# A gated delta rule on one NeuronCore: how the other stages' matmul columns are dealt out between the steps of its recurrence

## The chip, the core and the metric

One core of a Trainium2 chip runs the whole program; nothing else runs beside it. The metric is the device time of one execution in microseconds (us), and lower is better. The kernel before takes 4035.74 us, the median of three runs (4035.33 to 4039.92).

The core has five engines, each with a queue of its own that is worked off in order: TensorE (PE) for matmuls and transposes, with its weight loads as a row of their own (PEld); VectorE (DVE); ScalarE (ACT); GpSimd (POOL); and SyncE (SP), whose queue only issues DMAs.

## What is computed

Three layers follow each other on x of 4 x 512 tokens with 512 channels, all in float32. The change lies in the first one, a gated delta rule with 16 heads of 128 x 128 state:

```
q, k, v = silu(conv4(x @ W.T))              # causal convolution over 4 tokens, per channel
g, beta = exp(-exp(A_log) * softplus(a + dt_bias)), sigmoid(b)
q, k    = l2norm(q), l2norm(k)              # per head
for t in range(512):                        # per sequence and head, state S is 128 x 128
    error = v[t] - g[t] * (S.T @ k[t])
    S     = g[t] * S + outer(k[t], beta[t] * error)
    o[t]  = S.T @ q[t]
o = rmsnorm(o) * norm_w * silu(x @ Wg.T)    # rmsnorm over all heads
x = x + o @ Wo.T
```

Cross attention with fake quantisation follows, then causal attention and a mixture of 8 experts. They stay as they are, apart from what is said of counts below.

## The kernel before

**Pairs.** The recurrence is computed in chunks of 128 tokens, four to a sequence (`TB`), for two heads at a time (`HG`). Sequence and two heads make a *pair* `m`; there are 32 (`NP`). A pair passes through these generators, each of which yields between pieces of work:

- `stage1(m)` (L508) projects k and q, runs the convolution (`conv`, L483: four matmuls of 512 columns at L489, ScalarE at L497, three VectorE instructions at L500, silu on ScalarE at L503), transposes k (L532), takes its norms (squares at L537; on GpSimd a power at L544 and the products L545 to L548), scales the decay matrix `em` with them on ScalarE (`scale`, L383), multiplies k by k (L562) and writes the matrix `at` (L565) to DRAM (L566), multiplies q by k (L585), and sums q's squares (L594). The inverse of q's norm is formed on GpSimd (L608, L609).
- `stage2_inverse(m)` (L622) inverts the 32 x 32 diagonal blocks in 31 steps of two instructions (L630, L631), on VectorE for even `m` and on GpSimd for odd `m`, and stores and reloads them as `T` and `X`.
- `stage2_values(m)` (L646) projects v and the gate `gs` (silu at L493), and stores q's inverse norms (L651).
- `stage3(m)` (L676) is the recurrence itself. It first joins the blocks of the inverse to 128 x 128 in four small rounds of matmuls (L690/L691, L700/L702, L713, L722), with copies out of PSUM between them: of the copies after the first two rounds, L693, L704 and L706 are on VectorE, L694 and L705 on ScalarE, two instructions each to a pair. Then it loads q's inverse norms, broadcast to all partitions (`rrow`, L728), and multiplies the two gates by them on GpSimd (L731). Then come the four chunks `c`, each a chain from PE to another engine and back: state times k (L744), `r` on VectorE (L746), the inverse times `r` (L753), `u` copied by ScalarE (L755), the state's increment (L763), the new state (L766 on ScalarE for `c` = 0, else L768 on VectorE), and the output (L771, L773). At the end VectorE multiplies the output by norm weight and gate (`og`, L782, the reader of `gs`) and by q's inverse norms (L786), ScalarE squares it (L790) and GpSimd adds it up (L791).
- `output(m)` (L796) multiplies `og` by Wo (L811) and adds on VectorE (L816). After a sequence's last pair it also ends the sequence. `prologue(b)` (L387) prepares a sequence.

**Order.** While `stage3(m)` runs, the loop at L906 hands out the work of other pairs: `output(m - 1)`, `stage1(m + 2)`, `stage2_values(m + 1)`, `stage2_inverse(m + 1)`, and in one pair of eight `prologue`. `turns` (L170) gives each of them one or two steps (the number beside it) for every one of the 15 yields of `stage3(m)`, without regard to how much TensorE work a step holds:

```
rest = turns(*rest)
for _ in stage3(m):
    next(rest, None)
run(rest)
```

This sets the order in which instructions are traced. The framework then schedules: an instruction that it takes to be ready earlier may go ahead of another on its engine, so the order of the built program is near to this one and not the same. In the built program every engine's queue is fixed and runs in order. PSUM tiles of the projections and joins come from a pool of four (`p_b`), those of the recurrence from a pool of two (`p_s`).

**The rest.** The first pair's stages run before the loop. After the loop, cross attention and causal attention are interleaved tile by tile by `weave` (L145), which uses counts of steps from the table `steps` (L142); the experts follow. `cross(0)` alone runs in the loop, beside the last pair.

Of the kernel before, what the change touches and what calls it, by code (L numbers as in the profile page):

```python
# [33 lines left out]
ALU = mybir.AluOpType  # L34
# [64 lines left out]
def decoder(ctx: ExitStack, tc: tile.TileContext, a: dict, out: bass.AP):  # L99
# [42 lines left out]
    steps = {"first": 15, "cross": 30, "qkv": 15, "rest_of": 3, "route": 8}  # L142
    steps.update((f"attention{c}", n) for c, n in enumerate((28, 32, 44, 48)))

    def weave(*gs):  # L145
# [4 lines left out]
        while todo:  # L150
            t = min(todo)
            try:
                next(t[3])
                t[5] += 1
                t[0] += t[1]
            except StopIteration:
                steps[t[4]] = max(t[5], 1)
                todo.remove(t)
            yield

# [27 lines left out]
    def transposed(src, pool, name, bufs=2):  # L188

        tp = p_b.tile([P, KD, P], F32, name="pb")  # L190
        for kd in range(KD):
            nc.tensor.transpose(tp[:, kd, :], src[:, kd * P : (kd + 1) * P], ident)
# [26 lines left out]
    def cross(i):  # L219
# [11 lines left out]
        for kd in range(KD):  # L231
            nc.tensor.matmul(pq, xT[:, kd, :], wq[:, kd, :], start=kd == 0, stop=kd == KD - 1)
# [11 lines left out]
        def scores(g0, r0, out):  # L244
# [3 lines left out]
            for g in range(2):  # L248
                for r in range(2):
                    rs = slice((r0 + r) * HD2, (r0 + r + 1) * HD2)  # L250
                    nc.tensor.matmul(ps[r][:, g, :], qT[rs, g0 + g, :], x_kT[rs, g0 + g, :], start=True, stop=True)
# [18 lines left out]
        def turned(e, out):  # L270

            for r in range(2):
                tp = p_b.tile([P, 2, 2, P], F32, name="pb")
                for g in range(2):
                    for kt in range(2):
                        nc.tensor.transpose(tp[:, g, kt, :], e[:, 2 * r + g, kt * P : (kt + 1) * P], ident)
# [5 lines left out]
        def weighted(g0, eTs):  # L282

            pa = p_b.tile([P, 2, P], F32, name="pb")
            for g in range(2):
                for kt in range(2):
                    for r in range(4):
                        h = 4 * (g0 + g) + r
                        nc.tensor.matmul(pa[r * HD2 : (r + 1) * HD2, g, :], x_val[:, kt, h * HD2 : (h + 1) * HD2], eTs[r][:, g, kt, :], start=kt == 0, stop=kt == 1)
# [13 lines left out]
        for kd in range(KD):  # L303
            nc.tensor.matmul(pw, aT[:, kd, :], wpj[:, kd, :], start=kd == 0, stop=kd == KD - 1)
# [7 lines left out]
    with ExitStack() as st:  # L312
# [74 lines left out]
        def prologue(b):  # L387
# [8 lines left out]
            for c, t in enumerate(x):  # L396
# [5 lines left out]
                for kd in range(KD):  # L402
                    nc.tensor.transpose(tp[:, kd, :], t[:, kd * P : (kd + 1) * P], ident)
# [3 lines left out]
            for c in range(TB):  # L407
                for kd in range(KD):
                    nc.tensor.matmul(pab[:, c, :], xnT[:, kd, c * P : (c + 1) * P], wab[:, kd, :], start=kd == 0, stop=kd == KD - 1)
# [28 lines left out]
            for n, m in enumerate((C_UP, C_LO, C_ONE)):  # L438
                nc.tensor.matmul(pg[:, n, :], tab_a[:, m, :], lgf, start=True, stop=True)
# [21 lines left out]
            nc.tensor.transpose(tp[:, 0, :], w.rearrange("p h i -> p (h i)"), ident)  # L461
            nc.tensor.transpose(tp[:, 1, :], gam.rearrange("p h i -> p (h i)"), ident)
# [20 lines left out]
        def conv(b, hg, p, m, wt, dst):  # L483
# [4 lines left out]
            for kd in range(KD):  # L488
                nc.tensor.matmul(pj, wt[:, kd, p * P : (p + 1) * P], xnT[:, kd, :], start=kd == 0, stop=kd == KD - 1)  # L489
# [18 lines left out]
        def stage1(m):  # L508
# [20 lines left out]
            for p in range(HG):  # L529
                tp = p_b.tile([P, TB, P], F32, name="pb")  # L530
                for c in range(TB):
                    nc.tensor.transpose(tp[:, c, :], kT[p][:, c * P : (c + 1) * P], ident)  # L532
# [24 lines left out]
            for p in range(HG):  # L557
                scale(em[p], em[p], ee, p)
                pk = p_b.tile([P, TB, P], F32, name="pb")
                for c in range(TB):  # L560
                    k_ = kT[p][:, c * P : (c + 1) * P]
                    nc.tensor.matmul(pk[:, c, :], k_, k_, start=True, stop=True)  # L562
# [9 lines left out]
            for p in range(HG):  # L572
# [10 lines left out]
                for c in range(TB):  # L583
                    cs = slice(c * P, (c + 1) * P)
                    nc.tensor.matmul(pq[:, c, :], kT[p][:, cs], q[:, cs], start=True, stop=True)  # L585
# [7 lines left out]
            for p in range(HG):  # L593
                nc.tensor.matmul(pss[p * 32 : (p + 1) * 32, :], tab_a[:, C_ONE, 0:32], sq[p], start=True, stop=True)  # L594
# [51 lines left out]
        def stage2_values(m):  # L646
# [6 lines left out]
            for p in range(HG):  # L653
# [3 lines left out]
                for c in range(TB):  # L657
                    nc.tensor.transpose(tp[:, c, :], t[:, c * P : (c + 1) * P], ident)
# [17 lines left out]
        def stage3(m):  # L676
# [11 lines left out]
            for c in range(TB):  # L688
                for p in range(HG):
                    nc.tensor.matmul(py[lo[p], c, :], ats[p][:, c, 32:64], Ts[p][:, c, 0:32], start=True, stop=True)  # L690
                    nc.tensor.matmul(py[hi[p], c, :], ats[p][:, c, 96:128], Ts[p][:, c, 64:96], start=True, stop=True)  # L691
            for p in range(HG):
                nc.vector.tensor_copy(Yd[p][32:64, :, 0:32], py[lo[p]])  # L693
# [3 lines left out]
            for c in range(TB):  # L697
                for p in range(HG):

                    nc.tensor.matmul(px[half[p], c, 64:96], Xs[p][:, c, 32:96], Yd[p][:, c, 0:32], start=True, stop=True)  # L700
                for p in range(HG):
                    nc.tensor.matmul(px[half[p], c, 0:64], Yd[p][:, c, :], odd(Xs[p][:, c, :]), start=True, stop=True)  # L702
# [747 lines left out]
```

## Time and profile before

| what | value |
| --- | --- |
| median of three runs | 4035.74 us |
| the profiled execution's own time | 4042.91 us |
| span of its first to its last instruction | 4041.2 us |
| first join matmul (L690) of the first and of the last pair | 150.5 us and 2114.3 us |
| PE, DVE, ACT, POOL busy over the span | 88%, 55%, 38%, 34% |
| granted TensorE clock over the span | 0.930 of full |

How to read the profile: times are us from the span's start, unless marked ns. A group of instructions is named by its line, engine, operation and tile, as out<-in; the arrow in `<-DVE r L746` names what ended a wait. A float32 matmul appears as two instructions and a transpose as one. "Half clock" below is a stretch in which the granted TensorE clock is 0.50.

### The profile page before, as it was taken

To read this page: it belongs to the slowest core of one execution; us is meant where nothing else is said; L and a number is where in the kernel's file an instruction comes from. 1 tells how busy PE (TensorE), PEld (TensorE's weight loads), DVE (VectorE), ACT (ScalarE), POOL (GpSimd) and SP (SyncE) were. 2 spreads that over 40 slices of the span, in tenths; PEclk is the share of its full clock that TensorE was granted. 3 is DMA by queue.
4 is the path that set the end of the run, shared out by engine and by line. 5 is a ranking of instruction groups with operands and counts; after the bars stand their busy time and mean duration, and the time that the engine had idled before them with its cause. 6 is when DMAs were issued, how large, how long until landed. Compare 5 with 4: busy or idle time off the path is not lost. (4 is left out here: it accounts for less than half of the span.)

```text
span 4041.2 us, 50395 instructions
## 1 busy us (share of the span) xinstructions
PE 3555.1 (88%) x17170; PEld 2069.9 (51%) x17170; DVE 2220.7 (55%) x5115; ACT 1523.5 (38%) x4190; POOL 1370.0 (34%) x1941
## 2 busy tenths in 40 slices
PE   5898888988998898988898899979998998898797
PEld 3455555555555555555555455545554555455343
DVE  5566656766567755767555555445544554444211
ACT  2433434344433343343433344434443444343121
POOL 1453455434453354434552211121112111211342
PEclk7899899999999999999998899989998999899898
DMA  5334333343334333243334433443334443446344
GB/s 158 104 85 114 97 100 110 102 120 95 105 86 129 107 104 104 74 141 94 102 111 138 142 123 123 123 123 123 123 123 123 129 127 112 125 156 204 76 83 91
DMA packets 391888, 465.66 MB, mean 115 GB/s; under 512 B 128451, under 2 KB 242115, under 8 KB 391440
## 3 DMA queue, kind: packets, MB, share of 16 engines
q1 hardware_dynamic: 380080, 438.03, 36.4%
q0 software_dynamic: 10112, 21.58, 2.9%
q8 instruction: 137, 2.24, 0.2%
q10 hardware_dynamic: 1440, 2.84, 0.2%
q14 instruction: 119, 0.97, 0.1%
HBM read 401.76 MB, written 64.81 MB: 115 GB/s over the span
## 5 line engine op out<-in xcount | busy, mean ns | idle before, releaser
L489 PE MATMUL pb<-xnT,w 128*128 128x512 f32 x2048 | 955.8, 606 | 0.0
L489 PEld LDWEIGHTS pb<-xnT,w 128*128 128x128 f32 x2048 | 382.4, 196 | 424.9 <-issue 420.8
L500 DVE SCALAR_TENSOR_TENSOR cv<-pb,pp,cv 128x511 f32<-128x511 f32 (+2 forms) x576 | 427.6, 742 | 156.6 <-ACT cv L497 144.3
L1049 PE MATMUL pb<-c_q,hT 128*128 128x512 f32 x768 | 370.9, 625 | 0.2 <-ACT hT L194 0.2
L630 POOL TENSOR_TENSOR iW<-iA,iT 32x31 f32<-32x31 f32 (+15 forms) x496 | 249.7, 504 | 211.2 <-DMA iA<-at_d 141.2
L811 PE MATMUL pb<-wot,og 128*128 128x512 f32 x512 | 267.1, 647 | 31.8 <-DVE og L782 26.5
L631 POOL TENSOR_TENSOR iT<-iT,iW 32x31 f32<-32x31 f32 (+15 forms) x496 | 275.1, 555 | 38.9
L1113 PE MATMUL ps<-kT,qT 128*128 128x128 f32 x1280 | 205.2, 310 | 72.4 <-ACT e L1119 72.1
L1153 PE MATMUL po<-c_o,oT 128*128 128x512 f32 x512 | 247.0, 617 | 21.2 <-DVE oT L1137 11.2
L497 ACT ACTIVATE cv<-pb,pp 128x512 f32<-128x512 f32 x192 | 148.1, 771 | 264.4 <-PE pb L489 263.9
L1113 PEld LDWEIGHTS ps<-kT,qT 128*128 128x128 f32 x1280 | 183.8, 217 | 113.0 <-ACT e L1119 92.6
L1049 PEld LDWEIGHTS pb<-c_q,hT 128*128 128x128 f32 x768 | 147.0, 201 | 163.4 <-issue 160.3
L1119 ACT ACTIVATE e<-ps,nm,rq 128x128 f32<-128x128 f32 (+3 forms) x256 | 157.5, 621 | 181.8 <-DVE nm L1117 136.8
L630 DVE TENSOR_TENSOR iW<-iA,iT 32x31 f32<-32x31 f32 (+15 forms) x496 | 177.1, 357 | 14.0 <-DMA iA<-at_d 2.4
L631 DVE TENSOR_TENSOR iT<-iT,iW 32x31 f32<-32x31 f32 (+15 forms) x496 | 178.0, 359 | 11.9
L1136 PE MATMUL po<-eT,val 128*128 128x512 f32 x320 | 168.3, 620 | 15.2 <-ACT eT L1134 11.3
L258 ACT ACTIVATE x_e<-pb,nm 128x256 f32<-128x256 f32 x256 | 118.2, 474 | 149.1 <-DVE nm L255 145.6
L544 POOL TENSOR_TENSOR rk<-ss,mhalf 128x8 f32<-128x8 f32 x32 | 53.0, 1658 | 322.8 <-DVE ss L543 322.8
L263 POOL TENSOR_SCALAR x_e<-x_e 128x1024 f32<-128x1024 f32 x64 | 68.0, 1063 | 259.0 <-ACT x_e L258 141.0
L565 DVE SCALAR_TENSOR_TENSOR at<-pb,em 128x512 f32<-128x512 f32 x64 | 44.3, 692 | 200.9 <-ACT em L383 200.5
L1153 PEld LDWEIGHTS po<-c_o,oT 128*128 128x128 f32 x512 | 92.6, 196 | 118.7 <-issue 80.9
L982 POOL TENSOR_TENSOR rope_s<-q,tab 128x128 f32<-128x128 f32 x64 | 35.3, 552 | 332.1 <-DVE q L1079 246.7
(323 smaller groups left out, 6708.5 us busy)
## 6 DMA issues: line engine op xcount, KB each, us to landing
c_o<-in_c_wo_dram SPq DMA_DIRECT2D x128, 512.0 KB, 4.3
c_q<-in_c_wq_dram SPq DMA_DIRECT2D x128, 512.0 KB, 4.7
w<-in_a_w_dram SPq DMA_DIRECT2D x124, 512.0 KB, 3.9
row<-g_d SPq DMA_DIRECT2D x64, 512.0 KB, 4.0
at_d<-at SPq DMA_DIRECT2D x64, 256.0 KB, 4.1
T<-t_d SPq DMA_DIRECT2D x32, 512.0 KB, 6.1
X<-x_d SPq DMA_DIRECT2D x32, 512.0 KB, 6.7
rrow<-r_d SPq DMA_DIRECT2D x32, 512.0 KB, 4.7
```

The source lines that it names most:

```text
L258: nc.scalar.activation(e[:, n, :], ps[r][:, g, :], AF.Exp, bias=nm[:, n : n + 1], accum_out=ssum[:, n : n + 1])
L489: nc.tensor.matmul(pj, wt[:, kd, p * P : (p + 1) * P], xnT[:, kd, :], start=kd == 0, stop=kd == KD - 1)
L497: nc.scalar.activation(ac, pj, AF.Identity, bias=cb[:, m, h : h + 1], scale=cw[:, m, h, 3:4])
L500: nc.vector.scalar_tensor_tensor(ac[:, j:], pj[:, : S - j], cw[:, m, h, 3 - j : 4 - j], ac[:, j:], ALU.mult, ALU.add)
L630: eng.tensor_tensor(u, A[:, i, i + 1 :].unsqueeze(2).to_broadcast([nb, n, w]), T[:, i, :w].unsqueeze(1).to_broadcast([nb, n, w]), ALU.mult)
L631: eng.tensor_tensor(T[:, i + 1 :, :w], T[:, i + 1 :, :w], u, ALU.add)
L811: nc.tensor.matmul(pw, og[p][:, c * P : (c + 1) * P], wot[:, p, :], start=p == 0, stop=p == HG - 1)
L1049: nc.tensor.matmul(pj, hT[:, kd, :], w[:, kd % 2, :], start=kd == 0, stop=kd == KD - 1)
L1113: nc.tensor.matmul(ps[:, m, k * P : (k + 1) * P], qT[g][:, n + m, :], kT[:, g, :], start=True, stop=True)
L1119: nc.scalar.activation(e[n + m][:, :nk], ps[:, m, :nk], AF.Exp, bias=nm[:, n + m : n + m + 1], scale=rq, accum_out=es[:, n + m : n + m + 1])
L1136: nc.tensor.matmul(po, val[:, g, :], eT, start=k == 0, stop=k == c)
L1153: nc.tensor.matmul(pw, oT[:, h + m, :], w[:, m, :], start=h + m == 0, stop=h + m == H3 - 1)
```

## The change

1. The loop no longer uses `turns`. New wrappers `matmul` and `transpose` issue the same instruction and add its columns to a counter: a matmul its output columns (scaled by the width of its weights over 128), a transpose half of them. `spread` runs `stage3(m)`, and after each of its yields lets the other generators go on until the counted columns reach that yield's share, n sixteenths of the total. The total is the one counted the last time that the same set of generators ran, or 40,000 the first time. Among the generators the next step goes to the one that is furthest behind its own time table, from a begin to an end as shares of the pair.
2. The copies L693, L704 and L706 move from VectorE to ScalarE.
3. The gates' multiplication by q's inverse norms (L731, two GpSimd instructions) is issued after the chunks `c` = 1 and `c` = 2 instead of before the recurrence.

Every other line that the diff touches has only `nc.tensor.matmul` or `nc.tensor.transpose` replaced by the wrapper.

```diff
     steps = {"first": 15, "cross": 30, "qkv": 15, "rest_of": 3, "route": 8}
+    steps.update(stage1=27, values=14, inverse=33, output=4, end=16, prologue=14, stage3=16)
...
+    spent = [0.0]
+
+    def matmul(dst, w, x, **flags):
+        nc.tensor.matmul(dst, w, x, **flags)
+        spent[0] += float(np.prod(dst.shape[1:])) * (w.shape[1] / P)
+
+    def transpose(dst, src, i):
+        nc.tensor.transpose(dst, src, i)
+        spent[0] += dst.shape[1] / 2
+
+    cost = {}
+
+    def spread(main, kind, rest):
+        todo = [[b, n, (e - b) / steps[k], 0, g, k] for n, (g, k, b, e) in enumerate(rest)]
+        key = (kind, *(k for _, k, _, _ in rest))
+        total, others = cost.get(key, 4.0e4), 0.0
+
+        def one():
+            nonlocal others
+            t, was = min(todo, key=lambda t: t[:2]), spent[0]
+            try:
+                next(t[4])
+                t[0] += t[2]
+                t[3] += 1
+            except StopIteration:
+                steps[t[5]] = max(t[3], 1)
+                todo.remove(t)
+            others += spent[0] - was
+
+        n = 0
+        for _ in main:
+            n += 1
+            while todo and others < total * n / (steps[kind] + 1):
+                one()
+        while todo:
+            one()
+        steps[kind], cost[key] = n, others
...
             for p in range(HG):
-                nc.vector.tensor_copy(Yd[p][32:64, :, 0:32], py[lo[p]])
+                nc.scalar.copy(Yd[p][32:64, :, 0:32], py[lo[p]])
                 nc.scalar.copy(Yd[p][96:128, :, 32:64], py[hi[p]])
...
             for p in range(HG):
-                nc.vector.tensor_copy(Ts[p][32:64, :, 0:32], px[lo[p], :, 64:96])
+                nc.scalar.copy(Ts[p][32:64, :, 0:32], px[lo[p], :, 64:96])
                 nc.scalar.copy(Xs[p][0:32, :, 32:64], px[lo[p], :, 0:32])
-                nc.vector.tensor_copy(Xs[p][64:96, :, 96:128], px[hi[p], :, 32:64])
+                nc.scalar.copy(Xs[p][64:96, :, 96:128], px[hi[p], :, 32:64])
...
-            for p in range(HG):
-                nc.gpsimd.tensor_tensor(gs[p], gs[p], rb[p], ALU.mult)
...
                 st_ = nst
+                if 0 < c <= HG:
+                    nc.gpsimd.tensor_tensor(gs[c - 1], gs[c - 1], rb[c - 1], ALU.mult)
                 yield
...
             if m == NP - 1:
...
-                rest.append((cross(0), 2))
+                rest.append((cross(0), "cross", 0.0, 1.0))
             if m:
-                rest.append((output(m - 1), 1))
+                rest.append((output(m - 1), "end" if m % NHG == 0 else "output", 0.06, 0.6 if m % NHG == 0 else 0.4))
...
-                rest.append((stage1(m + 2), 2))
+                rest.append((stage1(m + 2), "stage1", 0.0, 0.95))
             if m + 1 < NP:
-                rest.append((stage2_values(m + 1), 1))
-                rest.append((stage2_inverse(m + 1), 2))
+                rest.append((stage2_values(m + 1), "values", 0.0, 0.95))
+                rest.append((stage2_inverse(m + 1), "inverse", 0.0, 0.9))
             if (m + 4) % NHG == 0 and (m + 4) // NHG < B:
-                rest.append((prologue((m + 4) // NHG), 1))
-            rest = turns(*rest)
-            for _ in stage3(m):
-                next(rest, None)
-            run(rest)
+                rest.append((prologue((m + 4) // NHG), "prologue", 0.0, 0.9))
+            spread(stage3(m), "stage3", rest)
```

## The prediction

> **What bounds the kernel now.** I read the page first, then the loop over pairs by windows, then PE's waits inside it, and last the timeline at the costliest waits.
>
> ```profile
> PE 3555.1 (88%) x17170; PEld 2069.9 (51%) x17170; DVE 2220.7 (55%) x5115; ACT 1523.5 (38%) x4190; POOL 1370.0 (34%) x1941
> ```
>
> PE is the busiest engine by far, so time is gained only where PE idles or runs at a lower clock. The windows view cuts out the loop from the first pair's start to the last but one's end, 30 pairs, and four single pairs (13 to 16); the columns are the stretch, its length, then busy us of PE, PEld, DVE, ACT and POOL, granted clock and DMA.
>
> ```profile
> 150.50:2078.40 1927.90, 1730.55 (x9057) 1026.08 (x9056) 1253.47 (x2616) 777.00 (x2176) 894.26 (x1346) 0.94 0.36 102
> 989.80:1051.80 62.00, 56.81 (x301) 33.23 (x303) 41.24 (x88) 23.88 (x70) 22.68 (x40) 0.94 0.34 93
> 1051.80:1116.30 64.50, 57.32 (x301) 34.11 (x300) 40.93 (x86) 24.65 (x71) 33.48 (x50) 0.95 0.33 99
> 1178.80:1245.70 66.90, 59.31 (x305) 36.27 (x304) 42.02 (x92) 25.10 (x71) 37.49 (x55) 0.90 0.42 127
> ```
>
> A pair takes 1927.9 / 30 = 64.3 us. PE idles 1927.9 - 1730.6 = 197 us, 6.6 us a pair. A clock of 0.94 between the two values 1.00 and 0.50 means half clock for 12% of the loop, some 225 us. If PE is busy in it, that costs up to half of it, about 112 us, 3.7 us a pair. What remains is about 54 us a pair of PE work at full clock. The change takes none of it away: 54 is the floor, and 197 + 112 = 309 us is the most that it can win. Now PE's waits, within the loop (waiter, what ended the wait, us, times, longest):
>
> ```profile
> PE ps L763 <- ACT u L755: 47.6, 13, 6.1
> PE ps L753 <- DVE r L746: 38.6, 41, 2.0
> PE pb L811 <- DVE og L782: 26.5, 27, 1.0
> PE pb L713 <- DVE cv L500: 22.6, 13, 2.3
> PE ps L744 <- DVE state L768: 18.4, 10, 8.6
> PE pb L409 <- ACT xnT L404: 14.7, 3, 5.6
> PE po L771 <- ACT u L755: 9.6, 27, 0.4
> ```
>
> Nearly all is latency of `stage3`: a step hands over to another engine, and PE has no foreign work behind it. The timeline of PE in pair 13 shows the common form:
>
> ```profile
> 1028.12 0.61 PE L763 MATMUL ps<-u,kdec 128*128 128x128 f32 x4
> ...
> 1029.46 0.61 PE L744 MATMUL ps<-state,kT 128*128 128x128 f32 x4
> 1031.55 0.49 PE L753 MATMUL ps<-r,X 128*128 128x128 f32 x2 [1.48 <-DVE r L746]
> 1032.40 0.50 PE L771 MATMUL po<-pt,u 128*128 128x128 f32 x2 [0.35 <-ACT u L755]
> ```
>
> Between L763 and the last L771 stands not one projection. The largest waits have another origin, seen on three engines in pair 16:
>
> ```profile
> 1206.14 1.96 POOL L635 COPY iA<-iT 32x1024 f32<-32x1024 f32 x1
> ...
> 1213.74 1.65 POOL L544 TENSOR_TENSOR rk<-ss,mhalf 128x8 f32<-128x8 f32 x1
> ```
>
> ```profile
> 1216.02 2.44 ACT L383 ACTIVATE em<-em,ee 128x128 f32<-128x128 f32 x8 [10.01 <-POOL ee L546]
> ```
>
> ```profile
> 1219.33 1.23 PE L763 MATMUL ps<-u,kdec 128*128 128x128 f32 x4 [6.10 <-ACT u L755]
> ```
>
> GpSimd finishes an inverse, adds up, multiplies the gates, and only then takes the power at L544; ScalarE stands 10 us at `em` for it, and the copy of `u` stands behind `em`. This returns in the even pairs, whose GpSimd holds the other pair's inverse. In the timeline 13 gaps of PE in the loop are longer than 3.4 us, most of them of this kind; in between, the odd pairs lose 5 to 6 us in small gaps.
>
> **The clock.** The loop has 40 stretches at half clock, 28 of them 3.4 us long. Cut into steps of 3.4 us, 41 steps at full clock are followed by half clock; PE was busy for at most 58% of each, and two small gaps in one step were enough. The Trainium skill, page "TensorE: Matmul & The Clock Gate", Part 1, says that the clock falls after an idle window of about 3.4 us, and advises against idle gaps longer than about 3. By that rule only the 13 long gaps would count, and a change that closes small gaps would win no clock at all; the traced steps say otherwise, so I go by the 58%.
>
> **Part 1, the equal shares.** The order of the built programs shows PE's queue. Before, the columns between a pair's steps are 4096 and 2048 between the joins' rounds, 3072, 1024, then 256 between the first L753 and L763, then about 1536, 2048, 2048, *nothing* from the second L763 through the third L753 and L763, and 4864 and 3584 at the end. Nothing stands between the last L773 and the next pair's join. After, in the 22 ordinary pairs (all but 0, 1, 4, 8, 12, 16, 20, 24, 30, 31), they are 2048, 1024, 2048, 1024, 2048, 1024, 1536, 1280, 1536, 1536, 1280, nothing from the third L763 to the fourth chunk's first L753, 3584, 1024, and 3584 after the last L773. 512 columns take 0.86 us (two L489 at 0.43 in the timeline). Step by step:
>
> - `og` (26.5 us): 3584 columns, 6 us, now stand before the join, and `output` comes after the third join round. To 0.
> - `r` and `state` (38.6 + 18.4 = 57): chunks 1 and 2 get cover of 2.6 us against 0.34 for L746. The bare stretch moves from chunk 2 to chunk 3. VectorE's queue there is L500, L768, L500, L768, L500, L746, L746. L500 takes 0.74, L768 0.30, so the second state is ready 2.1 us after L763, under which 0.9 us of L771/L773 lie: 1.2 lost; then L500 and L746, 1.1, less the second L744: about 0.8. That is 2.0 a pair, at least 0 if the L500s are done, at most 3.7 (pair 9 shows 2.27 and pair 13 1.48 at such steps). With less in pairs that have stalled before: 50 us, a gain of only 7.
> - `u` at L763 (47.6): the stall at `em` moves from chunk 1 to chunk 2. From the second k transpose to the waiting L763 PE has 9.7 us of work before and 11.2 after, so each of 15 even pairs saves 1.5 at most. I take 2.4 us left in each: 36. Bounds: 0, and 4.4 (the mean of these gaps now) x 15 = 66.
> - `u` at L771 (9.6): covered by 1024 columns. 5.
> - `xnT` (14.7, three pairs with a prologue): part of the same `em` stall. 12.
> - The first time a set of generators runs, 40,000 columns are assumed for about 24,600, so pairs 0, 1, 4, 8 and 30 run out of foreign work in chunks 2 and 3: no gain there.
>
> **Part 2, the copies.** 6 x 0.28 us a pair leave VectorE, 6 x 0.25 come to ScalarE (40% busy in the loop). L713's 22.6 us are waits behind L500 in VectorE's queue, and L704's own 2.8 go with them. ScalarE's six copies after the second round make 1.5 us, the fourth ends after 1.05, and 1024 columns, 1.72 us, lie over it. After the first round four copies, 1.0, lie under 3.4. I keep 3 us. If ScalarE is late by a silu (0.63) and a conv start (0.77), it costs 1.2 x 31 = 37 us.
>
> **Part 3, the gates.** Two of 1.25 us leave their place behind L635 and now stand within the inverse, after step 25 of 31. The same instructions stand ahead of L544, so I count 0. What it costs if the load of `rrow` is late is the fourth rival.
>
> **Sum.** Idle: 0 + 50 + 36 + 5 + 12 + 3 and 15 for the small remainder = 121, against 197: 76 won. Half clock: an odd pair now loses 5 to 6 us in two clusters, afterwards 2 to 3 in one, which is at the 58% limit; I take 0.7 stretches of 3.4 us in each of 15, cost (0.7 x 3.4 / 2) x 15 = 18. Even pairs keep their long gap and two stretches, 3.4 x 15 = 51, special pairs 20: 89 against 112, 23 won. Together 99 us. Outside the loop PE's order before the first join is unchanged, and the tiles after it differ in a few swaps: 0. 4042.9 - 99 = 3944 for the profiled execution, which lies 7.2 above the median; **3937** as the median.
>
> **Rivals.**
>
> 1. *The clock takes most of it.* If the bare stretch of chunk 3 still drops the clock in each pair and even pairs lose their full 4.4 us, idle is 150 and half clock stays: 47 won, 3989. For it: one cluster of 2 to 3 us is enough in pairs 10 and 11 now. Against it: it stands alone now. 0.18.
> 2. *The cover is complete.* If L500 is early in chunk 3 and the even pairs arrive after `u`, idle falls to some 60 and half clock to 40: 137 + 92 = 229 at most; middle 190, 3846. For it: GpSimd has no gates left after the inverse, 2.5 us. 0.17.
> 3. *It does not do what it says* (the scheduler, not the tracing, sets the order): 4036. The order of the built program speaks against it. 0.05.
> 4. *Slower: the gates block GpSimd.* If `rrow` lands late, GpSimd stands at the gate with a quarter of the inverse, L635 and L544 behind it, so `em`, `u` and PE follow. By my sum GpSimd gets there 20 us after the join. In pair 16 `rrow` landed 32.5 us after it: 12 us x 15 even pairs + clock, about 205 lost against 99 won: 4145. It decides from 99 / 15 = 6.6 us of lateness on. For it: 33.9 us of waits at L731 for `rrow` now. Against: SP's load of `rrow` stood behind the store of the inverse there, and in the built program it stands ahead. 0.10.
>
> **Numbers.** Forecast 0.50 (own range 3890 to 3975), rivals 0.18, 0.17, 0.05, 0.10. The range of 3845 to 4005 takes in rival 1, most of 2, and leaves out 3 and 4 and the end of 2. About 0.2% (8 us) can be told from no change: faster 0.85, same 0.05, slower 0.10.
>
> **What would show it.** Right: the waits at L811 for `og` and at L713 gone; L753 waits once a pair, in chunk 3; pairs of 60 to 62 us, even ones longer; half clock in the loop near 180 us. Wrong: GpSimd waiting at the gates for `rrow`; L713 waiting for ScalarE; pairs of different parity alike.

## The result, and the profile after

The changed kernel takes 4077.49 us (median of four runs, 4073.19 to 4080.05), the kernel before 4037.83 us beside it on the same chip (4035.33 to 4042.45). The ratio is 1.0096, with a 95% interval of 1.0078 to 1.0113: slower by 1%, where 2.4% less was forecast. The profiled execution took 4077.71 us, its span 4075.6 us.

The page's line of engines, of the kernel after:

```profile
PE 3538.4 (87%) x17170; PEld 2027.8 (50%) x17170; DVE 2148.0 (53%) x4923; ACT 1594.6 (39%) x4379; POOL 1382.8 (34%) x1941
```

PE does the same 17170 instructions, and 192 copies have left VectorE (5115 instructions before). The windows view of the kernel after, cut as in the prediction: 30 pairs from the first pair's start, then pairs 13 to 16 (columns: stretch, length, busy us of PE, PEld, DVE, ACT and POOL, granted clock, DMA).

```profile
152.05:2103.50 1951.45, 1703.53 (x9059) 977.19 (x9058) 1188.99 (x2441) 846.03 (x2355) 909.83 (x1350) 0.95 0.34 102
998.30:1059.90 61.60, 55.49 (x297) 31.36 (x296) 42.84 (x84) 27.22 (x77) 22.40 (x37) 0.97 0.32 88
1059.90:1130.00 70.10, 58.42 (x299) 33.25 (x298) 36.68 (x71) 27.55 (x77) 39.51 (x54) 0.93 0.35 105
1130.00:1189.40 59.40, 54.50 (x299) 30.51 (x298) 41.32 (x83) 27.04 (x77) 20.13 (x33) 1.00 0.32 89
1189.40:1262.90 73.50, 59.10 (x309) 34.81 (x309) 42.02 (x86) 27.39 (x77) 43.76 (x61) 0.91 0.43 137
```

Odd pairs (13 and 15) got shorter, 62.0 to 61.6 and 62.5 to 59.4 us, and even ones longer, 64.5 to 70.1 and 66.9 to 73.5. Over the whole loop, from the first to the last pair's first join, the 14 ordinary odd pairs went from a mean of 62.0 to 60.3 us, the 8 ordinary even ones from 64.1 to 69.5. The loop became 22.9 us longer (1963.5 to 1986.4); of the rest of the span's 34.4, 1.6 us came before it and 9.9 after its last pair began. In the loop PE idles 252.8 us against 199.4, while half clock fell from 225.3 to 182.7 us. The clock moved as forecast; the idle time moved the other way. Split by parity over the 30 pairs, the idle time went from 82.6 to 79.1 us in the 15 odd pairs and from 114.8 to 168.9 in the 15 even ones, half clock from 81.9 to 17.1 us in the odd and from 143.4 to 163.8 in the even ones. So the odd pairs got shorter by the clock, hardly by less idle time.

PE's waits within the 30 pairs of the kernel after. Matmuls and transposes show their wrappers' lines here, L165 and L169, so one goes by the tiles; L785 is the `r` of L746, L544 the silu of L503, L765 the fourth round's copy to X.

```profile
PE ps L165 <- DVE r L785: 69.3, 53, 8.8
PE pb L165 <- ACT qh L544: 67.1, 26, 7.1
PE pb L169 <- ACT cv L544: 31.8, 23, 8.4
PE ps L165 <- DVE state L807: 24.4, 51, 4.8
PE ps L165 <- ACT X L765: 16.8, 13, 4.5
PE pb L165 <- DVE xa L857: 15.8, 17, 2.3
PE ps L165 <- ACT u L794: 5.0, 3, 3.3
```

The waits at `og` (26.5 us before) and behind the second round of the join (22.6) are gone, those at `u` (47.6) nearly. In their place `r` costs 69 us instead of 39, and three waits are new: q's product (L585) for its own silu, 67 us against 3, v's transposes (L658) for theirs, 32 against none, and the first step of the chunks for X, 17 against none.

The stall at `r` and the wait at q's product are both seen in even pair 14. The timeline of the kernel after (start, duration, engine and line; in brackets the idle time before and what ended it):

```profile
1091.57 1.96 POOL L676 COPY iA<-iT 32x1024 f32<-32x1024 f32 x1
1093.61 1.64 POOL L585 TENSOR_TENSOR rk<-ss,mhalf 128x8 f32<-128x8 f32 x1
...
1095.88 1.86 ACT L424 ACTIVATE em<-em,ee 128x128 f32<-128x128 f32 x6 [7.71 <-POOL ee L587]
...
1098.44 0.75 DVE L541 SCALAR_TENSOR_TENSOR cv<-pb,pp,cv 128x511 f32<-128x511 f32 x1 [9.82 <-ACT cv L538]
1099.11 0.68 DVE L606 SCALAR_TENSOR_TENSOR at<-pb,em 128x512 f32<-128x512 f32 x1
1099.70 0.60 DVE L785 SCALAR_TENSOR_TENSOR r<-ps,ngam,vn 128x128 f32<-128x128 f32 x2
1100.10 1.22 PE L165 MATMUL ps<-r,X 128*128 128x128 f32 x4 [5.43 <-DVE r L785]
```

GpSimd's inverse still ends just before the power, as before, and `em` waits for it. But VectorE's queue now holds `r` of chunk 2 behind a conv and `at`, both of which hang on that `em`: the stall has moved from `u` to `r`, and grown. Some 10 us later, in the same pair:

```profile
1110.52 0.18 DVE L671 TENSOR_TENSOR iW<-iA,iT 32x31 f32<-32x31 f32 x1 [1.21 <-DMA iA<-at_d]
...
1117.78 0.73 DVE L541 SCALAR_TENSOR_TENSOR cv<-pb,pp,cv 128x511 f32<-128x511 f32 x1
1117.86 0.60 ACT L534 ACTIVATE gs<-pb 128x512 f32<-128x512 f32 x1 [1.01 <-PE pb L165]
...
1121.93 0.63 ACT L544 ACTIVATE qh<-cv 128x512 f32<-128x512 f32 x1 [3.48 <-DVE cv L541]
...
1122.62 1.84 PE L165 MATMUL pb<-qh,kT 128*128 128x128 f32 x8 [3.90 <-ACT qh L544]
```

From 1110.5 to 1117.8 VectorE does eleven steps of the *next* even pair's inverse, which the scheduler has put ahead of the second q head's conv; the conv, the silu and q's product come after them, and PE has run out of columns by then.

### The profile page after: what moved, and what is told of

It reads as the page before. It is cut to its first block, busy times and chain, and to the rows that moved or that the text cites. A ratio compares the mean times of both kernels' runs of the same rounds, so it can differ in the third digit from the quotient of the medians.

```text
span 4075.6 us, 50385 instructions
## 1 busy us (share of the span) xinstructions
PE 3538.4 (87%) x17170; PEld 2027.8 (50%) x17170; DVE 2148.0 (53%) x4923; ACT 1594.6 (39%) x4379; POOL 1382.8 (34%) x1941
## 5 line engine op out<-in xcount | busy, mean ns | idle before, releaser
L165 PE MATMUL pb<-xnT,w 128*128 128x512 f32 x2048 | 995.9, 620 | 18.9 <-DVE xa L857 13.9
L165 PEld LDWEIGHTS pb<-xnT,w 128*128 128x128 f32 x2048 | 378.1, 198 | 400.7 <-issue 367.0
L165 PE MATMUL pb<-c_q,hT 128*128 128x512 f32 x768 | 373.9, 629 | 0.7 <-ACT x_e L299 0.7
L165 PE MATMUL ps<-kT,qT 128*128 128x128 f32 x1280 | 210.6, 315 | 75.2 <-ACT e L1157 74.8
L165 PE MATMUL po<-c_o,oT 128*128 128x512 f32 x512 | 248.1, 619 | 20.1 <-DVE oT L1175 11.3
L165 PE MATMUL pb<-wot,og 128*128 128x512 f32 x512 | 250.9, 615 | 9.7 <-ACT X L765 3.1
L165 PEld LDWEIGHTS ps<-kT,qT 128*128 128x128 f32 x1280 | 188.6, 222 | 116.2 <-ACT e L1157 96.6
L165 PEld LDWEIGHTS pb<-c_q,hT 128*128 128x128 f32 x768 | 147.9, 203 | 166.2 <-issue 162.6
L672 DVE TENSOR_TENSOR iT<-iT,iW 32x31 f32<-32x31 f32 (+15 forms) x496 | 192.5, 388 | 13.0
L617 POOL TENSOR_TENSOR qg<-qh,row 128x512 f32<-128x512 f32 x64 | 82.5, 1291 | 321.2 <-issue 226.2
L165 PE MATMUL po<-eT,val 128*128 128x512 f32 x320 | 168.4, 620 | 13.9 <-ACT eT L1172 10.7
L585 POOL TENSOR_TENSOR rk<-ss,mhalf 128x8 f32<-128x8 f32 x32 | 52.8, 1651 | 347.5 <-DVE ss L584 346.6
L165 PE MATMUL pb<-qh,kT 128*128 128x128 f32 x512 | 87.5, 323 | 74.8 <-ACT qh L544 74.8
L165 PEld LDWEIGHTS po<-c_o,oT 128*128 128x128 f32 x512 | 92.7, 196 | 118.3 <-issue 81.1
```

The lines of the kernel that those rows point to most:

```text
L165: nc.tensor.matmul(dst, w, x, **flags)
L585: nc.gpsimd.tensor_tensor(rk, ss, mhalf[:, 0 : HG * TB], ALU.pow)
L617: nc.gpsimd.tensor_tensor(g, q, mb[p], ALU.mult)
L672: eng.tensor_tensor(T[:, i + 1 :, :w], T[:, i + 1 :, :w], u, ALU.add)
```

## The experiments

Each run's time is a median beside runs of the kernel before on the same chip (4036 to 4039 us); ratios are to that, with 95% intervals. Lines in the diffs are quoted without their wrappers. The texts on record name theories by letters and say what each means; A is the first theory: the shares keep the `em` stall and put dependent products right behind their own projections, and those waits are the loss.

**The parts.** e1 undoes part 2, e2 part 3, e3 makes parts 2 and 3 alone in the kernel before, e4 puts the true totals in place of 40,000:

```diff
-        total, others = cost.get(key, 4.0e4), 0.0
+        total, others = cost.get(key, known), 0.0   # 23808, 19712 or 12800; 23812, 25664, 15872 with end, prologue, cross
```

> The changed kernel with part 2 undone: L693, L704 and L706 are VectorE's again; equal shares and late gates stay. PE's queue is the same as in the changed kernel. Theory A (the equal shares are the loss; the copies help a little): L713 waits behind L500 again, some 25 us more than the changed kernel's 4077, so 4085 to 4105. Rival (the copies on ScalarE are the loss, its queue being late for everything behind them): below 4050.

Measured: 4083.9 us, 1.0123 (1.0096 to 1.0150), 6 more than the whole change, which the two intervals don't tell apart. Nothing waits behind L500 at the join here; the joins wait 15 us for `T` and 4 for `Y` instead, and the wait for X at the first step of the chunks falls from 16.8 to 2.9 us. So with the equal shares, part 2 trades one wait for another.

> The changed kernel with part 3 undone: the gates are multiplied before the recurrence again; equal shares and ScalarE's copies stay. PE's queue is the same as in the changed kernel. Theory A: the gates stand ahead of the power at L544 in either place, so within 15 us of the changed kernel, 4065 to 4095. Rival (the gates inside GpSimd's inverse make it late, as in the fourth rival of the prediction): below 4050.

Measured: 4073.2 us, 1.0100 (1.0071 to 1.0129): part 3 is worth nothing that can be told.

> The kernel before with parts 2 and 3 alone, dealt out by turns as before. PE's queue is that of the kernel before. Theory A: the waits of L713 go (25 us) and some of the clock with them, 3995 to 4025. Both rivals (part 2 or part 3 is the loss): 4045 or more.

Measured: 4029.3 us, 0.9987 (0.9974 to 1.0000), a small gain at most, short of what was expected: the wait at L713 fell from 22.6 to 9.1 us, but that at k's transposes (L532) rose from 6.6 to 21.3, and one of 9.5 us for `cv` appeared at the output projection. So the loss comes with part 1.

> The changed kernel, whose equal shares know the true total of columns from the first time on, instead of 40,000. It alters pairs 0, 1, 4, 8, 30 and 31. Theory A: pair 8 (12 us longer than before) and the passage to the attention (8 us longer) get some of it back: 4055 to 4070. Rival (first times do not matter, all of the loss is in the ordinary pairs): 4072 to 4082.

Measured: 4062.4 us, 1.0069 (1.0046 to 1.0093). The first-time default costs some 15 us of the 40, though the two intervals overlap a little.

**Taking single waits away.** e5 and e6 leave k's inverse norms out of `em`, in the kernel after and before; e7 lets the second head's product take the first head's q; e8 has both in the kernel after.

```diff
-                scale(em[p], em[p], ee, p)
+                scale(em[p], em[p], flat(beta), p)
```
```diff
-                    matmul(pq[:, c, :], kT[p][:, cs], q[:, cs], start=True, stop=True)
+                    matmul(pq[:, c, :], kT[p][:, cs], qs0[0][:, cs], start=True, stop=True)
```

> The changed kernel, with em scaled by beta alone, which is ready long before, instead of by ee: ScalarE no longer waits for GpSimd's power. It leaves the inverse norms of k out of em; every instruction and PE's queue stay. Theory A (the changed kernel loses most in the even pairs, where r stands in VectorE's queue behind at, at waits for em, and em for GpSimd): the 5.4 to 7.3 us of wait in 15 even pairs go, with half clock behind them, 100 to 130 us, so 3945 to 3980. Rival (a queue as such is full, so that another wait takes the place): 4040 or more.

Measured: 4051.3 us, 1.0027 (1.0015 to 1.0038).

> The same edit in the kernel before (it leaves the inverse norms of k out of em). Theory A: its even pairs lose 4.4 us at u and some clock, so 70 to 95 us go: 3940 to 3965, less of a gain than in the changed kernel. Rival (the stall at em is alike in both kernels and no part of the difference): the gap of some 40 us between the two kernels stays.

Measured: 3995.9 us, 0.9887 (0.9863 to 0.9910).

> The changed kernel, whose second product of q and k takes the first head's q, so that PE no longer waits for the second head's silu at the pair's end. It leaves the second head's own q out of that product; the number of instructions and PE's queue stay. Theory A: the 67 us of waits at L585 go, and some half clock, 60 to 85 us: 3990 to 4017. Rival (what follows is late all the same, the wait reappears at the last projections or at the next join): 4060 or more.

Measured: 4049.5 us, 1.0022 (1.0006 to 1.0037); the waits came back at `r` (95 us), `cv` (41) and `xa` (31).

> The changed kernel with both edits of the two runs above (k's inverse norms left out of em, the second head's q left out of its product with k). Theory A: the gains add up to 160 to 215 us: 3860 to 3915, which is what the prediction thought the equal shares could win. Rival (one stall hides the other): no more than 20 us below the better of the two.

Measured: 4019.5 us, 0.9935 (0.9914 to 0.9956). All four lie 30 us and more above A's ranges: A named real waits, but not what they were worth. e5 lies in its rival's range, by which another wait takes the place; what took it is in e5's trace. SyncE stores `at` and loads it back for the even inverse, and VectorE stands at that inverse's first step (timeline of e5, pair 10):

```profile
832.79 1.59 SPq L607 DMA_DIRECT2D at_d<-at  x2
842.59 0.34 SPq L660 DMA_DIRECT2D iA<-at_d  x1
```
```profile
845.93 0.18 DVE L671 TENSOR_TENSOR iW<-iA,iT 32x31 f32<-32x31 f32 x1 [12.84 <-DMA iA<-at_d]
...
856.90 2.07 PE L626 MATMUL pb<-qh,kT 128*128 128x128 f32 x8 [14.41 <-ACT qh L544]
```

With no wait at `em`, the step stood at the head of VectorE's queue 12.8 us before its data came, with q's conv behind it. In the loop such waits made 110 us in e5, against 22 in the kernel after and 2 in the kernel before: the `em` stall had hidden them. The same exchange is in e6, where they made 87 us and PE's wait at `r` rose from 39 to 89. The account that the inverse's place in VectorE's queue sets the loss is theory C.

**VectorE's inverse.** e9 and e10 leave the even pairs' inverses out, e11 leaves out the `em` wait too; e12 keeps the whole computation and adds one dependence, so that the even inverse can't go ahead of q's convs. e13 adds it to the kernel before.

```diff
-            load_blocks(m, ats)
+            if m % 2 or m == 0:
+                load_blocks(m, ats)
...
                 sq.append(t)
+                if p == 1 and m % 2 == 0 and m:
+                    nc.scalar.copy(elim[0][0:1, 0, 0:1], t[0:1, 0:1])   # elim[0] holds iA
+                    load_blocks(m, ats)
```

> The changed kernel with VectorE's inverses (those of the even pairs) left out: their 62 steps and the load of iA are not done, the copy and stores stay, so the results of even pairs are not the reference's. Theory C: in the changed kernel the steps of the next even inverse stand in VectorE's queue before the second q head's conv (L500), and the first waits for iA; PE waits behind them at q's product (L585, 67 us) and at v's transposes (L617, 32 us). Then L585's waits fall below 15 us and the time to 3995-4030. Rival D: em alone, held by GpSimd's power, delays the chain, and the inverse only fills time that VectorE would idle; then L585 keeps over 45 us of waits and the time is 4055-4080.

Measured: 3997.4 us, 0.9899 (0.9874 to 0.9924). The time is C's, its sign is not: q's product still waits 46 us (67 before) and v's transposes 24.5 (32), so most of these two waits did not stand behind the inverse.

> The kernel before with the same left out. Theory C: before, q's product had little wait (2.9 us), so only some r waits at L753 behind the inverse's steps go: 4015-4037, a gain of at most 20 and less than half of what the changed kernel gains by the same edit. Rival D: the same small gain in both, within 10 us of each other.

Measured: 3979.1 us, 0.9853 (0.9834 to 0.9873). The kernel before gains 59 us, far more than the 20 at most that C gave it: the inverse disturbed that one as well. It did not do so by `r`, whose wait stayed. What went are the waits at L713 (22.6 us) and at k's transposes (6.6), and half clock fell from 225 to 181 us:

```profile
PE ps L767 <- ACT u L759: 48.1, 12, 5.3
PE ps L757 <- DVE r L750: 38.3, 30, 2.3
```

> The changed kernel with both left out: VectorE's inverses of the even pairs, and k's inverse norms in em (so em does not wait for GpSimd's power). Theory C: taking away the em wait alone gained only 26 us because the wait for iA and the inverse's steps took its place in VectorE's queue; with both gone the even pairs come near the odd pairs' 60.3 us from 69.5, 8 us in each of 14 pairs and as much in the special ones: 3900-3960. Rival D (something else in the even pairs, such as GpSimd's own inverse, sets their length): above 4000.

Measured: 3925.4 us, 0.9728 (0.9709 to 0.9748). Alone the two edits gained 26 and 80 us, together 152: each wait hides part of the other. The range was met.

> The changed kernel, whole computation, with one added dependence: in the even pairs a ScalarE copy of one element from the second q head's square into iA, and iA's load behind it, so that VectorE's inverse can't start before both q heads' convs are done. Theory C: L585's waits fall below 20 us, 4010-4045. Against it: the inverse now starts a third of a pair later and ends after the last recurrence step; if X then comes late to the even pairs' joins, 3 to 6 us in each of 15 pairs are lost there and the time is 4060-4120. Rival D: 4070-4085, with the waits at L585 unchanged.

Measured: 4012.9 us, 0.9935 (0.9910 to 0.9959). One order in VectorE's queue was worth 65 us of the changed kernel, and the changed kernel with it beats the one before by 0.65%, as C's range had it. But 46 us at q's product and 27 us at v's transposes stayed, against C's 20; what fell most is the wait at `r`, from 69 to 36 us.

> The kernel before with the same added dependence as in e12 (whole computation). Theory C: here q's product hardly waited (2.9 us) and the inverse's steps stood mostly after q's convs, so the dependence gains at most 25 us: 4010-4035, above e12's 4013 or near it; the equal shares and their dependent products set the rest. Rival E (the inverse's place costs both kernels alike, and the shares are worth nothing or less by themselves): 3970-3990, below e12.

Measured: 4074.7 us, 1.0090 (1.0073 to 1.0107), slower than either theory had it. The held inverse now stands in front of `r` (92 us of PE's waits for it, 39 before), and runs beside GpSimd's: see the last section. So e13 is no clean control of the shares.

**Distance between a projection and its product.** e14 is e12 with e4's totals. e15 shifts the shares, e16 moves GpSimd's gates and sums of squares to VectorE, e17 is e15 with the gates forced behind the power:

```diff
-                yield
+                yield from idle(6 if p else 1)      # e15: ahead of q's product
...
-                rest.append((stage1(m + 2), "stage1", 0.0, 0.95))
+                rest.append((stage1(m + 2), "stage1", 0.0, 0.85))
-                rest.append((stage2_values(m + 1), "values", 0.0, 0.95))
+                rest.append((stage2_values(m + 1), "values", 0.1, 1.0))
```
```diff
+                if c == 2:                          # e17: rrow's load and both gates, moved here
+                    t = w2.tile([P, HG, S], F32, name="rrow", bufs=1)
+                    if m + 2 in ees:
+                        nc.scalar.copy(t[0:1, 0, 0:1], ees[m + 2][0:1, 0:1])
```

> e12 with the true totals of columns in place of 40,000 the first time a set of generators runs, as in e4, which gained 15 us of the changed kernel. Both theories: 3990-4005, pairs 4 and 8 shorter.

Measured: 3983.8 us, 0.9866 (0.9849 to 0.9883), 6 us below the range.

> e14 with the shares shifted so that a head's projection and the product that depends on it come two shares apart: six empty steps ahead of the second q head's product, stage1 due at 0.85 and the values from 0.1 to 1.0. Theory C: the waits at q's product and at v's transposes (46 and 27 us in e12) fall below 15 us together, and with half clock the time is 3925-3965. Rival F (GpSimd's chain from one em to the next em, some 62 to 64 us, sets the even pairs, and these waits only fill it): 3975-4005, the wait coming back at em or at r.

Measured: 3975.1 us, 0.9853 (0.9828 to 0.9878). This is F's range, and as F said a wait came back, here at `state` (84.5 us). The two waits fell from 75 us in e14 to 31 together, yet PE idles 189 us in the loop, as in e14 (192): in 11 of the 15 even pairs one gap of 9 to 11 us is left. GpSimd's timeline of e15, pair 14, shows what is in front of the power:

```profile
1050.79 1.67 POOL L658 TENSOR_TENSOR rq<-rq,mhalf 128x8 f32<-128x8 f32 x1
1052.43 1.27 POOL L840 TENSOR_TENSOR acc<-acc,cv 128x512 f32<-128x512 f32 x1
1057.61 2.48 POOL L823 TENSOR_TENSOR gs<-gs,rrow 128x512 f32<-128x512 f32 x2 [3.91 <-DMA rrow<-r_d]
1060.05 1.65 POOL L589 TENSOR_TENSOR rk<-ss,mhalf 128x8 f32<-128x8 f32 x1
```

> e15 with GpSimd's gate products and the sums of squares of the gated output on VectorE (whole computation). Rival F: GpSimd has 5 us less a pair, its chain gets shorter and 20 to 50 us are gained on e15. Theory C: within 15 us of e15, or slower where VectorE's queue grows.

Measured: 4150.7 us, 1.0278 (1.0259 to 1.0297). The gates' wait for `rrow` went along to VectorE, where more stands behind it: 328 us in 14 times, up to 25.7 us at a time, and with it PE's projections (271 us of waits in 13 times).

> e15 with one more dependence (whole computation): rrow is loaded in the third step of the chunks, behind a ScalarE copy of one element of the next but one pair's ee into it, so GpSimd takes the power that em waits for before it waits for rrow and multiplies the gates. If the gates in front of the power are the price (rival 4 in small), the power comes some 6 us earlier in 14 even pairs, their gap falls from 9 to 3 us and their half clock with it: 3850-3920. If the inverse before it sets the time, nothing is gained: 3965-3985. If rrow now comes too late for the gated output of the pair, a new wait appears at L823/L827 and the time is above 3985.

Measured: 3901.1 us, 0.9664 (0.9648 to 0.9680): 74 us less than e15 from the place of one load and two GpSimd instructions, and 3.4% better than the kernel before, with the whole computation. The gaps of 9 to 11 us fell to 4 to 6, and the ordinary even pairs went from some 64 to 59 us. GpSimd now stands 289 us for `rrow`, against 100 in e15, but behind the power instead of in front of it. It is the best version found that computes everything.

**The shares alone.** The missing corner to e11: the kernel before, without even inverses and without the `em` wait.

> The kernel before with what e11 leaves out of the changed one left out: VectorE's inverses of the even pairs, and k's inverse norms in em. If the equal shares win by themselves (theory C), this stays 15 to 50 us above e11's 3925: 3940-3975, with og's wait at the output projection (26 us) and more half clock in it. If they win nothing even with both engines out of the way (rival E): 3900-3930.

Measured: 3804.9 us, 0.9429 (0.9413 to 0.9445), 120 us *below* e11. C's belief that the shares win once the two engines are out of the way falls. The windows of e18, for 30 pairs and pairs 13 to 15, and PE's waits in it (lines as in the kernel before up to L622, four more after):

```profile
152.57:1836.40 1683.83, 1627.62 (x9057) 951.36 (x9056) 953.46 (x1684) 783.01 (x2168) 883.97 (x1348) 1.00 0.39 116
886.39:940.64 54.25, 53.44 (x297) 31.01 (x297) 25.02 (x46) 22.69 (x66) 26.20 (x46) 1.00 0.33 96
940.64:995.90 55.26, 53.47 (x297) 31.01 (x296) 30.14 (x52) 25.21 (x71) 30.75 (x45) 1.00 0.39 117
995.90:1051.50 55.60, 53.75 (x298) 31.04 (x296) 31.63 (x53) 25.21 (x71) 28.48 (x46) 1.00 0.39 110
```
```profile
PE pb L815 <- DVE og L786: 25.5, 26, 1.0
PE po L775 <- ACT u L759: 9.6, 27, 0.4
PE ps L757 <- DVE r L750: 8.0, 30, 0.6
PE pb L585 <- ACT qh L503: 4.0, 8, 0.9
PE ps L748 <- DVE state L772: 2.6, 3, 0.9
```

and PE's waits of e11, the same cut out of the changed kernel:

```profile
PE pb L626 <- ACT qh L544: 50.6, 27, 8.5
PE ps L787 <- DVE state L811: 24.7, 52, 4.1
PE ps L796 <- ACT X L769: 20.5, 9, 3.5
PE ps L796 <- DVE r L789: 19.2, 32, 2.7
PE pb L856 <- ACT X L769: 5.8, 2, 3.0
```

PE's order in e18 is that of the kernel before but for a few swaps, with its bare stretch in chunk 2. Undisturbed, that order loses 1.8 us a pair, at full clock. The equal shares lose 2.8 us in e11's odd pairs and 4.7 in the ordinary even ones; over the 30 pairs PE idles 136 us in e11 and 56 in e18, and half clock is 79 against 10 us. The rows show where: q's product stands too near to its projection (50.6 us), `state` and `r` wait in three places rather than one, and X comes late. The last may belong to part 2, since without it (e1) X's wait was 2.9 us; part 2 was not undone in e11, so how the 120 us divide between the shares and the copies is open.

| left out | before | after | the change costs |
| --- | --- | --- | --- |
| nothing | 4037.8 | 4077.5 | 40 |
| even inverses (e10, e9) | 3979.1 | 3997.4 | 18 |
| `em`'s wait (e6, e5) | 3995.9 | 4051.3 | 55 |
| both (e18, e11) | 3804.9 | 3925.4 | 120 |

## Why the prediction was wrong

**The step that failed** is the reading of the waits: "Nearly all is latency of `stage3`: a step hands over to another engine, and PE has no foreign work behind it." The four longest waits of `stage3` that it listed, at L763, L753, L713 and L744, make 127 us in the kernel before. With nearly the same order on PE and the two stalls taken away, e18 has 11 us of them (8.0 at `r`, 2.6 at `state`, 0.3 at `u`, none at L713). Each edit alone leaves most: e10 still has 100 us of them and e6 115. So nine tenths were VectorE and ScalarE arriving late, not PE lacking columns, and what the two edits left out can't be covered from PE: the changed kernel has the wait at `r` and `state` at 94 us, 57 before. The prediction did see GpSimd's power behind L763's wait and L500 behind L713's, and took that at L763 as moved, not gone; at `r` and `state` (57 us, 10.6 in e18) it counted latency alone. What made them late: their queues hold instructions that wait for GpSimd's power or for an inverse, and the inverse's own steps. e18 leaves out those steps too, VectorE's busy time in the 30 pairs falls from 1253 to 953 us, and so it is not told apart how much was standing and how much was working. The line "L753 <- DVE r" says that `r` came last, not why. The prediction's own example shows it: in pair 13 of the kernel before the first `r` ended at 1031.5. VectorE had stood for `em`, and the conv that needs ScalarE came after it and in front of `r`:

```profile
1025.94 0.69 DVE L565 SCALAR_TENSOR_TENSOR at<-pb,em 128x512 f32<-128x512 f32 x1 [0.48 <-ACT em L383]
...
1030.49 0.75 DVE L500 SCALAR_TENSOR_TENSOR cv<-pb,pp,cv 128x511 f32<-128x511 f32 x1 [0.98 <-ACT cv L497]
1031.15 0.34 DVE L746 SCALAR_TENSOR_TENSOR r<-ps,ngam,vn 128x128 f32<-128x128 f32 x1
```

PE waited 1.48 us there. The same place in e18's pair 14, with the same order on VectorE, cost 0.22 us.

**The second step that failed** is the cover itself. The sum had 121 us of idle time left of 197; 248 were measured in the 30 pairs. `r` and `state` came to 44 us more than their term, `u` and `xnT` to 46 less, and the "15 for the small remainder" to more than 140, of which q's product and v's transposes are 99. New columns were counted as cover, and what those columns themselves wait for was put at nothing.

Point by point:

- *What bounds.* "54 us a pair of PE work at full clock" held: 53.5 us busy in e18's pairs.
- *`og`* to 0, *L713* to 3, *`u` at L771* to 5: right. The first two are gone, the third is 1.8. *`xnT`*, 14.7 to 12: gone as well.
- *`r` and `state`, 57 to 50*: 93.7. The stall of the even pairs went there.
- *`u` at L763, 47.6 to 36, 2.4 left in each even pair*: 5.0, but the stall reappears one step earlier, at `r`, with 5.4 us in pair 14. The estimate weighed the work of PE on both sides; it didn't look at what the scheduler had put before `r` in VectorE's queue.
- *15 for the small remainder*: q's product (67) and v's transposes (32) are in no term of the sum. The prediction counted columns as cover for `stage3`'s steps, and forgot that the columns have chains of their own, from projection to conv, silu and product: equal shares put the ends of those chains right behind their beginnings. e15 bears this out as far as the waits go (75 to 31 us); in time it gained 9 us, which the intervals don't tell from nothing. So what these chains cost in time is argued, not shown.
- *First-time totals, "no gain there"*: a loss, some 15 us in e4 and 29 from e12 to e14.
- *An odd pair loses "5 to 6 us", "afterwards 2 to 3"*: 5.5 us before, 5.3 after. What was won at `og` and the join went to q's product (22 us in the 15 odd pairs), `xa` (14) and v's transposes (9).
- *The clock, 23 won*: 225 to 183 us of half clock, against "near 180" forecast: right in sum, in part by luck. By the forecast's own terms the odd pairs should have kept 36 us and the others 142; they had 17 and 164. And 58% is no limit: in the kernel before, a step with PE busy for 43% (1985.06 to 1988.47) was followed by one at full clock, and e11 lost the clock after 65% (last section).
- *Part 2, 25 to 3 us and no more*: e1 gives it 6 us, within the noise. The cost bounded there (ScalarE late by a silu) is visible in another place: X comes late to the first L753, 16.8 us against 2.9 in e1.
- *Part 3, 0*: right (e2). *Rival 4*, gates blocking GpSimd, did not decide here: 20 us of such waits in the 30 pairs. But its mechanism was real: taking it away was worth 74 us to e15 (e17), and e16, which moves that wait to VectorE, is 176 us slower than e15. The rival's own sum is slightly off: 205 lost against 99 won gives 4142, not 4145.
- *Own signs*: half clock near 180 and the waits at `og` and L713 gone were right; "pairs of 60 to 62 us" held for the mean of the odd pairs alone (60.3). "L753 waits once a pair, in chunk 3" did not hold: most pairs wait in chunk 2 too, for some 0.5 us in the odd ones and up to 7.3 in the even ones. The even pairs were left to a remark ("even ones longer"), and they decided.

None of the four rivals has this form: a stall that is not PE's, kept and moved to a place with more behind it.

**Open.** Why half of the special pairs (8, 16, 24) got longer and 4, 12 and 20 shorter was followed only as far as e4's totals go. Of the 120 us that the change costs when both stalls are out, no single wait was taken away. e18's floor was not reached with the whole computation; the order of the kernel before, with its two stalls removed by other means than e13's, was not tried.

## What to carry to other kernels

A wait's releaser tells who came last; before buying cover on the waiting engine, read what stood before the releaser in its own queue, and whether that waits for a third engine or a DMA. Price a stall by removing it in *both* orders, and in pairs: here single removals were worth 26 and 80 us, both together 152, and in the kernel before 43, 59 and 232. Spreading columns evenly also moves producers close to their consumers: count the distance in each chain that is spread, not only in the one that is covered.

## What the hardware did that was not expected

**Two vector engines on one step.** In e13 VectorE's and GpSimd's inverses run at the same time. VectorE's multiplication of 32 x 135 elements takes 0.29 us in the 17 cases without a busy GpSimd beside it and 0.57 us (median) in the 15 with one; at 32 x 31 it is 0.18 (3 cases) against 0.70 us (29). GpSimd's own of 32 x 135 take 0.41 us in both kernels. In e13's pair 15 it looks like this:

```profile
1185.44 0.63 DVE L635 TENSOR_TENSOR iT<-iT,iW 32x60 f32<-32x60 f32 x1
1186.11 0.70 DVE L634 TENSOR_TENSOR iW<-iA,iT 32x31 f32<-32x31 f32 x1
```

In the kernel before no step of one inverse overlaps a step of the other; in e13 248 of VectorE's 992 do. The Trainium skill, page "SBUF — State Buffer", sections "Who interferes with whom" and "Summary: rules for kernel authors", says that a VectorE instruction with two SBUF inputs contends with a GpSimd instruction that reads SBUF, and that the later one is fully blocked until the first ends; a 0.18 us step that takes about as long as GpSimd's whole instruction (0.58 to 0.69 there) agrees with it.

**The clock falls without any long gap.** In e11's pair 13 the longest gap of a step of 3.41 us was 0.43 us, and PE was busy for 2.20 of it, 65%; half clock followed (windows of e11):

```profile
966.46:969.87 3.41, 3.41 (x21) 2.41 (x21) 1.57 (x3) 2.55 (x7) 0.00 (x0) 1.00 0.50 117
969.87:973.28 3.41, 2.20 (x13) 1.46 (x12) 2.69 (x7) 2.84 (x8) 2.17 (x8) 1.00 0.00 0
973.28:976.69 3.41, 3.41 (x10) 1.99 (x9) 0.00 (x0) 0.30 (x2) 2.94 (x7) 0.51 0.00 0
```

The prediction had 58% as the highest share of a step before a fall. The rule of an idle window on the Trainium skill's page "TensorE: Matmul & The Clock Gate", Part 1, doesn't cover this case: the longest gap here is an eighth of its 3.4 us.
